# A graph network's first norm and attention product by node blocks, ahead of a run-time branch, with the slot fills spread over the gathers

## The chip, the cores and the metric

The kernel runs on one core of one Trainium2 chip. The metric is the device time of one execution in microseconds (us). The engines are PE (TensorE, matrix products), DVE (VectorE), ACT (ScalarE), POOL (GpSimd) and SP (SyncE, which here only issues DMAs). Each engine works through its own list of instructions in order; waits between engines go over semaphores.

## What is computed

The reference is a stack of four pairs of a graph layer and a feed-forward layer over 3125 nodes of width 256 and 50000 edges sorted by destination. The change touches the first pair and the start of the second:

```python
x = x + _L0_gnn_ref(_layernorm(x, axis=-1), edge_index, L0_gnn_W, L0_gnn_att_src, L0_gnn_att_dst, ...)
x = x + _L0_ffn_ref(_layernorm(x, axis=-1)[None], L0_ffn_router_w, L0_ffn_w1, ...)[0]
x = x + _L1_gnn_ref(_layernorm(x, axis=-1), edge_index, edge_attr_64, L1_gnn_W1, ...)
...
# the first graph layer (8 heads of 32):
h = (x @ W).reshape(n, H, C)
a_src = jnp.einsum('nhc,hc->nh', h, att_src)
a_dst = jnp.einsum('nhc,hc->nh', h, att_dst)
e = a_src[src] + a_dst[dst]
e = jnp.where(e > 0, e, NEG_SLOPE * e)
...
alpha = ex / denom[dst]
msg = h[src] * alpha[..., None]
out = jax.ops.segment_sum(msg, dst, num_segments=n).reshape(n, H * C) + bias
```

## The kernel before, in words

Nodes lie in 25 tiles of 128 (`NT`), grouped in 7 blocks of four tiles, the last block of one (`BLOCKS`). Edges lie in 392 tiles of 128 (`ET`), worked in 28 groups of 14 (`GF`). A tile `x` of all nodes (25 x 256 floats in each of 128 partitions) stays in SBUF for the whole kernel.

The order of the first 700 us is this:

1. **Constants and loads.** x is loaded with two DMAs on SP's queue (L113, L114), the edges' node numbers and weights on ACT's queue (L122, L124).
2. **The flag** (L151 to L195). A fast form of the kernel holds if the edges' destinations fall into expected windows and the source nodes' counts into expected bounds. DVE works this out from the node numbers; for each of 26 node tiles it compares (L181) and ACT squares and sums (L182). The answer is `flag`, one integer.
3. **The first norm** (`layernorm(x, xn)`, `norm_tiles`): statistics of all 25 tiles (L244, L245), one chain of root and reciprocals for all (L226 to L237), then 25 scalings (L248).
4. **The branch.** Every engine reads `flag` (L2095), and the kernel goes on in the form for windows (`gat_gelu`, `mpnn_buckets`, and so on) or in a general form.
5. **`attention`**, in the branch: all of `xn` is transposed by PE (L262), multiplied by `W` (L738), copied to `hs` (L739); the scores of source and destination come from DVE by multiplying `hs` with the attention vectors and summing each head (L744, L746, five tiles at a time). The softmax's shift and the node's own edge follow (L751 to L762). `hs`, 264 floats a node (256 values and 8 scores), is stored in HBM as the table `h_tab` by one DMA (L763).
6. **Fills.** `zero_slots` writes zeros over `slot_x` (10.4 MB, one DMA, L198) and two edges of `rows_y` (L201); `zero_buckets` writes zeros over 25 pieces of `slot_r` (L207). All on SP's queue. `slot_x` is first written with data in the experts that follow, `slot_r` in `mpnn_buckets`.
7. **The edge groups** (`gat_gelu`). For each group POOL gathers the source rows from `h_tab`, 14 indirect DMAs (L293, tile `gw_m`, three buffers); SP loads the row of destination numbers (`dst_hot`, tile `w_row`, L397, one buffer); DVE makes 0/1 matrices of it (L405); PE fetches destination scores with them (L413); ACT and DVE make and apply the weights (L1045 to L1053); PE sums over edges into a window's nodes (L1070). At a node tile's first window its own row from `hs` is weighted and added (L1064 to L1069). Finished nodes get their norm and the router's choice (`consume`).
8. **The experts** (`sparse_experts`): 50 indirect stores into `slot_x`, then 32 tiles of 256 slots, each with two products, results scattered to `rows_y`. In the later expert layers (`sure=43`, `sure=34`) the last tiles are run only if a count read at run time asks for them.
9. **`mpnn_buckets`**: `prepare` takes the experts' two rows for each node of a block (`collect`, tile `se_g`, four tiles at a time, one buffer), adds them, norms and transposes; then edge groups are computed and POOL stores them into `slot_r` with 392 indirect DMAs.

A scheduler fixes the order of each engine's list when the kernel is built: among the instructions of a stretch without a branch it can put one ahead of another that stands earlier in the text, if its inputs are ready sooner. It does not move instructions over the branch. `issue_after` is an explicit edge against that, used in `sparse_experts`.

Of the kernel before, what the change touches and what calls it, by code (L numbers as in the profile page):

```python
# [8 lines left out]
F32 = mybir.dt.float32  # L9
# [8 lines left out]
P = 128  # L18
# [73 lines left out]
def gnn_ffn_kernel(ctx: ExitStack, tc: tile.TileContext, I: dict, out: bass.AP):  # L92
# [20 lines left out]
    nc.sync.dma_start(x[:, :NT - 1], I["x"][:(NT - 1) * P].rearrange("(t p) d -> p t d", p=P))  # L113
# [36 lines left out]
    with tc.tile_pool(name="win", bufs=1) as p, tc.tile_pool(name="win_ps", bufs=1, space=PSUM) as ps:  # L150
        wid = p.tile([P, ET], F32, name="win_w")  # L151
        for k in ("src", "dst"):
            colf[k] = p.tile([P, ET], F32, name=k + "_colw")
            V.tensor_copy(colf[k], col[k])
        for a, b, ts in RUNS:
            nc.gpsimd.memset(dloc[:, a:b], float(ts[0] * P))
            nc.gpsimd.memset(wid[:, a:b], float(len(ts) * P))
        V.tensor_tensor(dloc, colf["dst"], dloc, op=OP.subtract)
        V.tensor_tensor(wid, dloc, wid, op=OP.is_lt)
        V.scalar_tensor_tensor(wid, dloc, 0.0, wid, op0=OP.is_ge, op1=OP.mult)  # L160
        ok = p.tile([P, 1], F32, name="win_ok")
        V.tensor_reduce(ok, wid, AX.X, OP.min)
        col1 = p.tile([P, 1], F32, name="win_1")
        V.memset(col1, 1.0)
        pt = ps.tile([1, 1], F32, name="win_p")
        PE.matmul(pt, ok, col1, start=True, stop=True)
        okf = p.tile([1, 1], F32, name="win_f")
        V.tensor_scalar(okf, pt, P - 0.5, None, op0=OP.is_gt)


        V.tensor_scalar(stile, colf["src"], 1.0 / P, -(P - 1.0) / (2.0 * P), op0=OP.mult, op1=OP.add)
        V.tensor_scalar(stile, stile, 1.5 * 2.0 ** 23, 1.5 * 2.0 ** 23, op0=OP.add, op1=OP.subtract)
        nc.gpsimd.iota(wid, pattern=[[P, ET]], base=0, channel_multiplier=1, allow_small_or_imprecise_dtypes=True)
        V.tensor_scalar(wid, wid, E - 0.5, float(NT), op0=OP.is_ge, op1=OP.mult)
        V.tensor_tensor(stile, stile, wid, op=OP.max)
        V.scalar_tensor_tensor(sloc, stile, -float(P), colf["src"], op0=OP.mult, op1=OP.add)
        V.tensor_scalar(sloc, sloc, 1.0, None, op0=OP.add)
        rt = p.tile([P, NT + 1], F32, name="win_rt")
        for b in range(NT + 1):
            eq = p.tile([P, ET], F32, name="win_eq", bufs=3)  # L180
            V.tensor_scalar(eq, stile, float(b), None, op0=OP.is_equal)  # L181
            S.activation(eq, eq, AF.Square, accum_out=rt[:, b:b + 1])  # L182
        po, pc = (ps.tile([P, NT + 1], F32, name="win_p" + k) for k in "oc")
        PE.matmul(pc, ones, rt, start=True, stop=True)
        PE.matmul(po, upper, rt, start=True, stop=True)
        V.scalar_tensor_tensor(sadj, iota256[:, :NT + 1], float(BT * P), po, op0=OP.mult, op1=OP.add)
        V.tensor_scalar(sadj, sadj, -1.0, None, op0=OP.add)
        lo, hi = p.tile([1, NT], F32, name="win_lo"), p.tile([1, NT], F32, name="win_hi")
        for a, b in ((0, NT - 1), (NT - 1, NT)):
            V.tensor_scalar(hi[:, a:b], pc[0:1, a:b], B_TILES[a] * P + 0.5, None, op0=OP.is_lt)  # L190
            V.tensor_scalar(lo[:, a:b], pc[0:1, a:b], B_FULL[a] * P - 0.5, None, op0=OP.is_gt)
        V.tensor_tensor(lo, lo, hi, op=OP.mult)
        V.tensor_reduce(hi[:, 0:1], lo, AX.X, OP.min)
        V.tensor_tensor(okf, okf, hi[:, 0:1], op=OP.mult)
        V.tensor_copy(flag, okf)  # L195

    def zero_slots():
        nc.sync.dma_start(slot_x.rearrange("(a p) w -> p a w", p=P),  # L198
                          zero[:, :D + 1].unsqueeze(1).to_broadcast([P, SLOTS // P + 1, D + 1]))
        for k in range(2):  # L200
            nc.sync.dma_start(rows_y[k * NR + N:(k + 1) * NR], zero[:NR - N, :D])  # L201

    def zero_buckets(slot_r):
        for b in range(NT):
            n = B_TILES[b] - B_FULL[b]
            row = (b * BT + B_FULL[b]) * P
            nc.sync.dma_start(slot_r[row:row + n * P].rearrange("(k p) w -> p k w", p=P),  # L207
                              zero[:, :D + 1].unsqueeze(1).to_broadcast([P, n, D + 1]))

# [413 lines left out]
    def sparse_experts(hot, n, T, name, f, act, beside=iter(()), meanwhile=None, sure=None):  # L623
# [83 lines left out]
        def collect(pool, t0, nt):  # L707
            g = pool.tile([P, len(hot), 4, D], F32, name="se_g")[:, :, :nt]
# [14 lines left out]


    def attention(p, h_tab):


        hs = p.tile([P, NT, W], F32, name="hs")
        ad = p.tile([P, NT, 16], F32, name="ad")
        exs = p.tile([P, NT, 8], F32, name="exs")  # L730
        w = load_w(p, "L0_gnn_W")
        with transposed(xn), tc.tile_pool(name="gat_ps", bufs=3, space=PSUM) as ps, \
                tc.tile_pool(name="gat_t", bufs=2) as tp:
            att = {k: load_bc(tp, "L0_gnn_" + k, D) for k in ("att_src", "att_dst")}
            for t in range(NT):
                pt = ps.tile([P, D], F32, name="gat_p")
                for c in range(2):
                    PE.matmul(pt, xnT[:, c, t * P:(t + 1) * P], w[:, c], start=c == 0, stop=c == 1)  # L738
# [1462 lines left out]
```

## Time and profile before

| what | value |
|---|---|
| time, median of 3 runs | 5363.52 us (5352.59 to 5365.13) |
| the profiled execution, its own time | 5371.22 us |
| its span, first to last instruction | 5369.5 us |
| granted TensorE clock, mean | 0.844 |
| busy, share of the span: PE, DVE, POOL, ACT | 79%, 48%, 42%, 22% |
| DMA | 644.19 MB, mean 120 GB/s |
| gathers of `gw_m` on POOL | 392, 401.2 us busy, 1024 ns mean |
| SP's first `zero_slots` store issued; wait of the next one (L201) behind it | 38.38 us; 44.1 us |
| first load of `se_g` in `mpnn_buckets` | 915.18 us |

A row of the timeline gives start, duration, engine, line, operation, output and input tiles and a count; in brackets stands how long the engine was idle before it and what released it. A row by stretches gives the length, each engine's busy time with its instruction count, the granted TensorE clock, the DMA engines' busy share and GB/s. "issue" as releaser means that the profile shows nothing that was waited for. L12 is line 12 of the kernel.

### The profile page before, as it was taken

How to read it: one execution, taken by the hardware profiler on the slowest of the kernel's cores; microseconds unless marked ns; L12 is line 12 of the kernel's file. 1: busy time of each engine (PE TensorE's matmuls, PEld its weight loads, DVE VectorE, ACT ScalarE, POOL GpSimd, SP SyncE). 2: the span in 40 equal slices, each digit the busy share in tenths (PEclk: the TensorE clock that was granted, in tenths of full speed). 3: DMA queues.
4: the chain of work that ended last, by engine and by line, in shares of the span. 5: the costliest groups of instructions: out<-in, count | busy, mean ns of one | idle time of the engine just before them, and what ended most of it. 6: DMA issues, size and time to landing. Idle time of an engine off the chain costs nothing. (4 is left out here: it accounts for less than half of the span.)

```text
span 5369.5 us, 59465 instructions
## 1 busy us (share of the span) xinstructions
PE 4264.2 (79%) x19362; PEld 2844.8 (53%) x19362; DVE 2594.7 (48%) x9507; ACT 1176.0 (22%) x2327; POOL 2245.9 (42%) x2372
## 2 busy tenths in 40 slices
PE   2578738999979999583799999989787788775694
PEld 2466527455556666442566666655454344443483
DVE  6577637311144555436856766762333313336324
ACT  2001012222233333111333433453000100002121
POOL 1777644767710000133523333300777537771521
PEclk8778859888989999756899999998788758885797
DMA  7644437545442232144333333312333223330564
GB/s 200 198 151 150 129 110 235 188 141 166 163 140 71 89 98 79 32 150 134 121 95 104 104 106 96 96 44 85 107 104 105 77 73 104 104 105 21 174 214 135
DMA packets 338232, 644.19 MB, mean 120 GB/s; under 512 B 54675, under 2 KB 244087, under 8 KB 333559
## 3 DMA queue, kind: packets, MB, share of 16 engines
q1 hardware_dynamic: 219872, 335.77, 20.1%
q0 software_dynamic: 108480, 298.44, 18.2%
q10 hardware_dynamic: 9558, 6.01, 0.4%
q8 instruction: 163, 2.67, 0.2%
q14 instruction: 159, 1.29, 0.1%
HBM read 508.81 MB, written 131.23 MB: 119 GB/s over the span
## 5 line engine op out<-in xcount | busy, mean ns | idle before, releaser
L293 POOL DMA_INDIRECT hc_wm<-hc_tabc,src_col x784 | 749.3, 956 | 649.2 <-DMA w_L_gnn_c_w<-in_L_gnn_c_w 304.0
L377 PE MATMUL w_acc<-hc_wm,w_eq 128*128 128x256 f32 x2208 | 751.4, 467 | 203.7 <-DMA hc_wm<-hc_tabc,src_col 148.4
L377 PEld LDWEIGHTS w_acc<-hc_wm,w_eq 128*128 128x128 f32 x2208 | 438.9, 224 | 516.7 <-DVE w_eq L370 258.8
L370 DVE TENSOR_SCALAR w_eq<-iota,dloc,ew 128x128 f32<-128x128 f32 (+1 forms) x784 | 300.3, 385 | 748.0 <-PE w_acc L377 741.1
L293 POOL DMA_INDIRECT hb_r<-hy_x,src_col x392 | 386.4, 986 | 644.3 <-PE hb_acc L1869 390.1
L610 POOL DMA_INDIRECT slot_x<-xn,sl_i x125 | 122.1, 977 | 975.3 <-DVE sl_i L582 754.4
L610 POOL DMA_INDIRECT slot_r<-mq_r,bk_i x392 | 399.5, 1019 | 195.5 <-issue 93.5
L293 POOL DMA_INDIRECT gw_m<-gat_h,src_col x392 | 401.2, 1024 | 140.0 <-issue 123.5
L1070 PE MATMUL gw_acc<-gw_m,gw_eqt 128*128 128x264 f32 x1104 | 303.7, 436 | 97.7 <-issue 86.0
L1899 PE MATMUL hb_pc<-hb_parts,w_hot 128*128 128x257 bf16 x1656 | 270.3, 295 | 138.3 <-DVE hbe_a L1904 88.1
L610 POOL DMA_INDIRECT rows_y<-se_y,se_to x175 | 181.3, 1036 | 349.0 <-DVE se_y L694 181.9
L1193 PE MATMUL mq_pe<-a_L_gnn_W1T_c,mq_ea 64*128 64x256 f32 x784 | 300.0, 466 | 29.3 <-ACT mq_r L1195 14.7
L1070 PEld LDWEIGHTS gw_acc<-gw_m,gw_eqt 128*128 128x128 f32 x1104 | 232.6, 216 | 153.4 <-issue 90.2
L413 PEld LDWEIGHTS <-w_hot 128*128 128x128 bf16 x3312 | 187.2, 100 | 233.6 <-issue 197.8
L1869 PE MATMUL hb_acc<-hb_r,hb_eq 128*128 128x257 f32 x1104 | 290.9, 389 | 13.3 <-DVE hb_eq L1864 13.2
L1899 PEld LDWEIGHTS <-w_hot 128*128 128x128 bf16 x1656 | 159.9, 103 | 264.3 <-DVE hbe_a L1904 125.8
L413 PE MATMUL mq_pe<-mq_q,w_hot 128*128 128x256 bf16 x1656 | 272.8, 294 | 0.0
L405 DVE TENSOR_SCALAR w_hot<-w_row,node_id 128x1792 bf16<-128x1792 int32 (+13 forms) x183 | 151.7, 833 | 218.8 <-PE mq_pe L413 153.1
L1770 ACT ACTIVATE hb_h<-hb_ph,hb_o,hb_s 128x512 f32<-128x512 f32 (+1 forms) x224 | 162.7, 730 | 413.0 <-PE hb_ph L1768 412.8
L1869 PEld LDWEIGHTS hb_acc<-hb_r,hb_eq 128*128 128x128 f32 x1104 | 200.4, 194 | 76.7 <-issue 27.5
L688 PE MATMUL se_py<-se_w,se_h 128*128 128x256 f32 (+1 forms) x886 | 236.3, 412 | 1.1 <-ACT se_h L681 1.0
L679 PE MATMUL se_ph<-se_xT,se_w 128*128 128x256 f32 (+1 forms) x972 | 235.8, 392 | 0.5 <-DVE se_xT L662 0.5
(523 smaller groups left out, 7266.9 us busy)
## 6 DMA issues: line engine op xcount, KB each, us to landing
w_row<-in_dst_row SPq DMA_DIRECT2D x84, 896.0 KB, 5.2
mb_r<-slot_r SPq DMA_DIRECT2D x48, 1156.5 KB, 5.7
se_w<-in_L_ffn_lanes SPq DMA_DIRECT2D x34, 1026.0 KB, 5.4
hb_w<-in_L_ffn_W SPq DMA_DIRECT2D x112, 256.0 KB, 2.7
se_r<-slot_x SPq DMA_DIRECT2D x66, 257.0 KB, 3.6
se_w<-in_L_ffn_lanes SPq DMA_DIRECT2D x32, 513.0 KB, 5.0
se_g<-rows_y SPq DMA_DIRECT2D x30, 512.0 KB, 5.7
hb_w<-in_L_ffn_Wo SPq DMA_DIRECT2D x56, 256.0 KB, 2.8
```

Of the source, the lines that this page charges most:

```text
L293: nc.gpsimd.indirect_dma_start(out=dst, out_offset=None, in_=table, in_offset=bass.IndirectOffsetOnAxis(ap=idx, axis=0))
L370: V.tensor_scalar(eq[:, :n], iota256[:, :n], dloc[:, i:i + 1], scale[:, u:u + 1], op0=OP.is_equal, op1=OP.mult)
L377: PE.matmul(acc[t][:, :width], eq[:, k * P:(k + 1) * P], m[:, u, :width], start=i == W_FIRST[t], stop=i == W_LAST[t])
L413: PE.matmul(o, hot[t][:, u * P:(u + 1) * P], parts[:, t, k, :width], start=start and j == 0, stop=j == len(ops) - 1)
L610: d = nc.gpsimd.indirect_dma_start(out=table, in_=rows, in_offset=None, out_offset=bass.IndirectOffsetOnAxis(ap=idx, axis=0)).ins
L679: PE.matmul(ph[:fp], w[:, c * f + j * P:c * f + j * P + fp], xT[:, c], start=c == 0, stop=c == 1)
L688: PE.matmul(py[:, u], h[:kp, j, u * P:(u + 1) * P], w[:kp, o2 + j * D:o2 + (j + 1) * D], start=j == 0, stop=j == nj - 1)
L1070: PE.matmul(acc[t][:, :W], eq[:, k * P:(k + 1) * P], m[:, u], start=False, stop=i == W_LAST[t])
L1193: PE.matmul(pt[:, v], ea[:, (u + v) * P:(u + v + 1) * P], w1c, start=True, stop=False)
L1770: S.activation(o[:, j, :n], ph[:, :n], AF.Relu, bias=shift[i][:, e, j:j + 1], scale=scale[i][:, e, j:j + 1])
L1869: PE.matmul(acc[t][:, :D + 1], eq[:, k * P:(k + 1) * P], b[:, u], start=i == W_FIRST[t], stop=i == W_LAST[t])
L1899: PE.matmul(pc[:, :D + 1], hot[t][:, u * P:(u + 1) * P], parts[t][:, 0, k], start=z == 0, stop=z == len(ops) - 1)
```

## The change

x comes in seven DMAs, six of four tiles and the last part tile. The flag's work becomes a generator, `windows`, that stops at seven places. `attention` now stands ahead of the branch and goes over the blocks: norm of four tiles, transposes, product, copies, one store of the block's rows into the table, and after each block but the first two steps of the flag's work. The attention scores come out of the same product: the weight `W` is extended by 16 columns, `W` times the heads' vectors, made by PE at the start from the transposed weight and a block matrix laid out on the host. `hs` is not kept in SBUF; a node tile's own row is loaded again from the table. The fills become generators too: `slot_x` in 21 pieces of up to four tiles and `slot_r` in 25, one of each for each edge group. In `mpnn_buckets` the experts' rows are collected two tiles at a time. `ad` and `exs` (scores and own weights) live to the end of the kernel.

```diff
-    nc.sync.dma_start(x[:, :NT - 1], I["x"][:(NT - 1) * P].rearrange("(t p) d -> p t d", p=P))
+    for t0 in range(0, NT - 1, 4):
+        nc.sync.dma_start(x[:, t0:t0 + 4], I["x"][t0 * P:(t0 + 4) * P].rearrange("(t p) d -> p t d", p=P))
...
     def zero_slots():
-        nc.sync.dma_start(slot_x.rearrange("(a p) w -> p a w", p=P),
-                          zero[:, :D + 1].unsqueeze(1).to_broadcast([P, SLOTS // P + 1, D + 1]))
+
         for k in range(2):
             nc.sync.dma_start(rows_y[k * NR + N:(k + 1) * NR], zero[:NR - N, :D])
+        per = 4
+        for a in range(0, SLOTS // P + 1, per):
+            n = min(per, SLOTS // P + 1 - a)
+            nc.sync.dma_start(slot_x[a * P:(a + n) * P].rearrange("(a p) w -> p a w", p=P),
+                              zero[:, :D + 1].unsqueeze(1).to_broadcast([P, n, D + 1]))
+            yield
...
             nc.sync.dma_start(slot_r[row:row + n * P].rearrange("(k p) w -> p k w", p=P),
                               zero[:, :D + 1].unsqueeze(1).to_broadcast([P, n, D + 1]))
+            yield
...
-        def collect(pool, t0, nt):
-            g = pool.tile([P, len(hot), 4, D], F32, name="se_g")[:, :, :nt]
+        def collect(pool, t0, nt, size=4):
+            g = pool.tile([P, len(hot), size, D], F32, name="se_g")[:, :, :nt]
...
+    def windows(p, ps):
...
+        for b in range(NT + 1):
+            eq = p.tile([P, ET], F32, name="win_eq", bufs=3)
+            V.tensor_scalar(eq, stile, float(b), None, op0=OP.is_equal)
+            S.activation(eq, eq, AF.Square, accum_out=rt[:, b:b + 1])
+            if b % 4 == 3:
+                yield
...
-    def attention(p, h_tab):
...
+    h_tab0 = tc.dram_tile([NR, W], F32, name="gat_h")
+    ad = const.tile([P, NT, 16], F32, name="ad")
+    exs = const.tile([P, NT, 8], F32, name="exs")
+
+    def attention(beside):
...
+            w = p.tile([P, 2, D + 16], F32, name="at_w")
+            nc.scalar.dma_start(w[:, :, :D], I["L0_gnn_W"].rearrange("(k p) c -> p k c", p=P))
+            wT, heads = load_w(p, "L0_gnn_WT"), load_w(p, "L0_gnn_heads", 2, 16)
+            for k in range(2):
+                pt = pbt.tile([P, 512], F32, name="bt_p")
                 for c in range(2):
+                    PE.matmul(pt[:, :16], wT[:, c, k * P:(k + 1) * P], heads[:, c], start=c == 0, stop=c == 1)
+                V.tensor_copy(w[:, k, D:], pt[:, :16])
+            sc = p.tile([P, NT, 8], F32, name="at_sc")
+            for s, n in BLOCKS:
+                t0, nt = s // P, n // P
+                norm_tiles(bp, x, xn, t0, nt)
+                xT = block_transposed(bp, pbt, xn, t0, nt, "at_xT")
+                hs = bp.tile([P, 4, W], F32, name="at_hs")
+                for u in range(nt):
+                    pt = ps.tile([P, 512], F32, name="at_p")
+                    for c in range(2):
+                        PE.matmul(pt[:, :D + 16], xT[:, c, u * P:(u + 1) * P], w[:, c], start=c == 0, stop=c == 1)
+                    S.copy(hs[:, u], pt[:, :W])
+                    S.copy(ad[:, t0 + u, :8], pt[:, W:W + 8])
+                nc.sync.dma_start(node_rows(h_tab0)[:, t0:t0 + nt], hs[:, :nt])
+                V.tensor_copy(sc[:, t0:t0 + nt], hs[:, :nt, D:])
+                for _ in range(2 if s else 0):
+                    next(beside, None)
+            for _ in beside:
+                pass
...
     def gat_gelu(mp, slot_r, beside):
...
-                hs, ad, exs = attention(p, h_tab)
-                zero_slots()
-                zero_buckets(slot_r)
...
+                    fills = [zero_slots(), zero_buckets(slot_r)]
...
                         hot = dst_hot(ep, g, 1)
+                        for fill in fills:
+                            next(fill, None)
...
                                     own = bp.tile([P, W], F32, name="gw_own")
+                                    nc.sync.dma_start(own, h_tab[t * P:(t + 1) * P])
                                     V.tensor_tensor(own[:, :D].rearrange("p (h c) -> p h c", h=HEADS),
-                                                    hs[:, t, :D].rearrange("p (h c) -> p h c", h=HEADS),
+                                                    own[:, :D].rearrange("p (h c) -> p h c", h=HEADS),
...
-                g = collect(tp, t0, nt)
-                for u in range(nt):
-                    add(t0 + u, g[:, :, u])
+                for u0 in range(0, nt, 2):
+                    m = min(2, nt - u0)
+                    g = collect(tp, t0 + u0, m, 2)
+                    for u in range(m):
+                        add(t0 + u0 + u, g[:, :, u])
...
-    layernorm(x, xn)
+    with tc.tile_pool(name="win", bufs=1) as p, tc.tile_pool(name="win_ps", bufs=1, space=PSUM) as ps:
+        attention(windows(p, ps))
     in_windows = nc.values_load(flag[0:1, 0:1], min_val=0, max_val=1)
```

## The prediction

> **What bounds the kernel now.** I read the table by 50 us stretches first, then the timeline of the first 190 us, then SP's and POOL's waits, and last the stretch 898 to 1012 us, because the change also touches a load there. The page gives the span.
>
> ```profile
> span 5369.5 us, 59465 instructions
> ```
>
> By stretches (length, busy us of PE, PE loads, DVE, ACT, POOL with instruction counts, then granted clock, DMA share, GB/s):
>
> ```profile
> 50.00:100.00 50.00, 31.66 (x150) 27.41 (x150) 41.65 (x70) 14.34 (x33) 0.00 (x0) 0.85 0.86 222
> 100.00:150.00 50.00, 3.27 (x6) 1.55 (x6) 22.72 (x47) 0.37 (x1) 26.27 (x24) 0.53 0.96 275
> 150.00:200.00 50.00, 21.03 (x159) 17.48 (x160) 21.57 (x46) 1.13 (x4) 29.82 (x32) 0.62 0.68 209
> 186.00:648.00 462.00, 357.59 (x2819) 289.07 (x2815) 343.10 (x965) 43.46 (x96) 355.59 (x350) 0.83 0.50 154
> ```
>
> From 186 to 648 us POOL issues gathers without a break: it counts as 77% busy, but each 0.95 us gather is followed by a fixed 0.30 us, so it is full. PE (358/462 = 77%) and DVE (343/462 = 74%) are not. **POOL's 392 gathers set this stage**, and whatever lets the first one start earlier, or removes a hole in their row, comes off the end. The timeline shows what precedes them:
>
> ```profile
> 37.21 0.14 DVE L195 CAST flag<-win_f 1x1 int32<-1x1 f32 x1
> 37.44 0.75 DVE L244 BATCH_NORM_STATS2 ln_st<-x 128x6 f32<-128x256 f32 x2
> 104.72 1.49 DVE L746 TENSOR_REDUCE ad<-gat_tmp 128x40 f32<-128x1280 f32 x1
> 104.88 0.36 SPq L763 DMA_DIRECT2D gat_h<-hs  x1
> 105.29 50.34 SPq L207 DMA_DIRECT2D slot_r<-zero  x20
> 117.20 1.39 POOL L293 DMA_INDIRECT gw_m<-gat_h,src_col  x1 [9.95 <-DMA gat_h<-hs]
> 118.89 5.05 POOL L293 DMA_INDIRECT gw_m<-gat_h,src_col  x1 [0.30 <-issue]
> 155.81 16.29 SPq L397 DMA_DIRECT2D w_row<-in_dst_row  x2
> 170.57 1.15 DVE L405 TENSOR_SCALAR w_hot<-w_row,node_id 128x1792 bf16<-128x1792 int32 x1 [47.46 <-DMA w_row<-in_dst_row]
> 186.08 0.94 POOL L293 DMA_INDIRECT gw_m<-gat_h,src_col  x1 [11.04 <-issue]
> 647.58 0.95 POOL L293 DMA_INDIRECT gw_m<-gat_h,src_col  x1 [0.30 <-issue]
> ```
>
> The flag, the norm and the attention run one after another to 106 us, the table of 3.3 MB lands at 117. Then SP sits in the zero fills until 155.8, so the first row of node numbers (`w_row`), in program order behind the fills, makes DVE wait 47 us. POOL fills its three group buffers (42 gathers, the last at 174.10) and stops for 11.04 us. From 117.20 to 647.58 is 530.4 us for 391 steps. Undisturbed (186.08 to 647.58, 349 steps) a step takes 461.5/349 = 1.322 us, so 391 steps need 517.0: 13.4 us of the stage are holes, those 11 and the slow 5.05 us gather.
>
> **The change, part by part.** *The stretch before the gathers.* Removed: ten multiplies and ten reductions of 1.49 us (DVE rows L744, L746; issued 1.40 us apart, 28 us from 78.17 to 106.1), the wait of the norm for the flag, and the wait for the whole norm. Added: PE columns 256 to 272, 25 small ACT copies, 7 instead of one table stores, and small norm steps seven times. What each engine then has to do, from the rows:
> - DVE: statistics 10.0 (37.44 to 47.4), applying 8.2 (L248, 25 in 8.16), the chain of root and reciprocal 1.5 for each of 7 blocks (49.28 to 50.61 and 0.18) = 10.6, seven score copies of 0.2 = 1.4, the flag's work 16.7 (5.7 before the 26 compares, 26 x 0.36 = 9.4, tail 1.6). Sum 47.
> - ACT: 26 squares 13.4 (L182), 7 roots 1.5, 14 transposed copies 7.5, 25 copies of 0.37 = 9.3, 25 small ones of about 0.2 = 5, three table loads 3.8. Sum 40.5.
> - PE: 50 transposes 9.9 (L262, 3.06 + 6.88), products 22.4 (L738, 2.42 + 20.02) x 272/256 = 23.8, the weights' heads some 2. Sum 36 at the 0.9 clock of 60 to 80 us; at the 0.53 of 100 to 117, 36 x 0.9/0.53 = 61.
>
> These now overlap. DVE had its first column list at 3.77 and `dst` at 6.99, so a first part of x is there at about 6: 6 + 47 = 53 if DVE never waits. Behind its last part come one tile's transposes, copies, product and copy (0.7 + 1.0 + 0.9 + 0.6 = 3.2), the store (2 to 4; the 128 KB and 256 KB rows land in 2.2 to 2.8) and the branch (SP's first fill came 1.0 after the flag): **61 at best**. At worst PE bounds at half clock: the identity is there at 12.0, 12 + 61 + 7 = 80, and another 12 for the seven handovers DVE to ACT to DVE to PE to ACT (the same serial chain took 678.2 to 688, 10 us, for one block): **92**. I take 73, nearer the first: the busiest engine holds 47, and the flag's 16.7 us are there to fill the gaps. Gain 117.2 - 73 = **44.2** (bounds 25 to 56).
>
> The root alternates with the flag's squares on ACT. The row decides that this needs no table loads: the 125 squares of L1588 stand among roots and show none. The Trainium skill ("ScalarE: Activation LUTs", "Table sets: the hidden batching unit") says to batch by set and names relu, copy, identity and abs as present in all, not the square; by it, with its 2.66 us a switch, 14 switches would put 37 us on ACT and make it the bound, near my 92.
>
> The 16 to 25 bias additions that DVE now does while it waits move behind the branch; they have the 18 us before the first group is complete.
>
> *The fills.* 21 pieces of slot_x and 25 of slot_r (514 KB each but one) move from one burst to two a group. The first `w_row` comes before them in the program, so the 11 us stop and the slow second gather go: 530.4 becomes 517.0. The same 23 MB still pass SP: twenty pieces took 50.34 us beside gathers, 2.5 each. If the scheduler bunches them, `w_row` waits 2.5 for each piece ahead of it, and up to the old 13.4 comes back. I allow 3. Gain **10.4** (0 to 13.4). Bytes are no obstacle: two pieces in 18.5 us add 57 GB/s to the 154 there, and 275 was moved in 100 to 150 while gathers kept 1.25 us apart. Here the Trainium skill speaks against the change: "DMA: Bandwidth & Descriptors" ("Bandwidth") wants 1 MiB or more for 75% of peak. Big and small fills show little of it here: the stretches show 344 GB/s at 40 to 44 us with the single 10.4 MB fill and 313 at 130 to 156 with pieces and gathers; by the rule the sum would lose a few us more of the 10.4.
>
> *Own rows.* 25 loads of 132 KB replace reading SBUF. The 128.5 KB loads of L656 land in 2.3 us; SP can issue them one tile ahead, two buffers exist, and DVE and PE have 26% and 23% slack, 4.8 us of a group. Taken at 0; uncovered 25 x 2.3 = 57.
>
> *Experts' rows in two halves.* `collect` in `mpnn_buckets` now loads two tiles at a time into one buffer. For the first block the second load waits for the first's additions: the additions ran from 919.09 and loads take 3.8 at least, so +**4**, which the first POOL scatter (937.74) inherits. Later blocks are ahead of need: DVE waits there 7.4 to 7.75 us a group for POOL's scatters. Uncovered, six blocks add 6 x 3.8 = 23.
>
> *Split x load, constants kept for good*: nothing beyond the above.
>
> Sum: -44.2 - 10.4 + 4 = **-50.6**. The profiled execution took 5371.22 (span 5369.5), 7.7 above the median of 5363.52; so 5320.6 for it, and 5363.5 - 50.6 = **5313** for the median.
>
> **Rivals.** *Half is given back* (5339): the stretch ends at 92 and the holes stay: -25.2 - 0 + 4 = -21, 5342; with the holes half gone, 5336. For it: PE's clock was 0.53 when it worked in bits. Against: before, PE was at 0.94 within 10 us of its first transpose. *More is gained* (5297): start at 61, no hole: -56.2 - 13.4 + 4 = -65.6. Needs an almost unbroken DVE. *Own rows stall the stage* (slower): SP is one queue in order, and its waits at `w_row` sum to 158.8 us in 12 (13.2 each) behind DVE's compares alone. If each own row stands behind such a wait, DVE stops 25 x 13.2 = 330 us; 28 groups x 4.8 = 134 absorb the first part, 196 stay: 5313 + 196 = 5509. It decides from (134 + 50.6)/25 = 7.4 us a tile. Against: SP's list is built by readiness (it put the slot_x fill of L198 ahead of the earlier-written store L763), so own rows should go early. *Empty tiles passed over*: the diff holds no such code. `sure=43` and `sure=34` with their `If` are in both kernels, the first experts keep all 32 tiles; worth 0, already in the sum.
>
> **How the numbers follow.** Main case 0.68 (own range 5297 to 5330), more gained 0.11, half given back 0.14, stall 0.04, other scheduling in the rest that eats it all 0.03 (5360). The range 5288 to 5342 leaves out the stall, that last case and the edges, 2 in 10. Noise is about 0.3% = 16 us: faster means below 5347. Faster 0.91, same 0.05, slower 0.04.
>
> **What would show it.** First gather near 73 (61 to 92) and after the flag's cast; no `gat_tmp` rows; no POOL hole over 5 us in the first 60 us of gathers; `w_row` landed within 10 us of the first gather; last gather near 593; steps still 1.32 us; the first scatter of slot_r some 4 us later after the last rows_y scatter than before. Wrong if steps exceed 1.45, if DVE waits for `gw_own` loads, or if stages past 1000 us change length.

## The result, and the profile after

| | before | changed |
|---|---|---|
| median of 13 runs each, taken together | 5377.44 us (5342.88 to 5418.81) | 5325.73 us (5272.48 to 5353.44) |
| profiled execution, its span | 5369.5 us | 5315.8 us |
| granted clock of the profiled execution | 0.844 | 0.848 |

The ratio is 0.9898, with a 95% interval of 0.9867 to 0.9929: 1.0% less, some 55 us, and the interval excludes no change. The medians above differ by 51.7 us, since the ratio leaves out one execution of the changed kernel, that of 5353.44 us, which fell in a slower state. The prediction's 5313 against its 5363.5 is a ratio of 0.9906. The profiled execution took 5317.6 us.

The two traces by stages (start of the first instruction of a kind, us):

| mark | before | changed | difference |
|---|---|---|---|
| first gather of `gw_m` | 117.20 | 68.61 | -48.6 |
| last gather of `gw_m` | 647.58 | 596.65 | -50.9 |
| first scatter into `slot_x` | 710.27 | 659.59 | -50.7 |
| first load of `se_g` | 915.18 | 864.53 | -50.7 |
| first scatter into `slot_r` | 937.74 | 893.93 | -43.8 |
| last scatter into `slot_r` | 1507.54 | 1455.37 | -52.2 |
| end of the span | 5369.5 | 5315.8 | -53.7 |

Nearly all of the gain is made before the first gather. By stretches, the kernel after (length, busy us of PE, PE loads, DVE, ACT, POOL with instruction counts, then granted clock, DMA share, GB/s):

```profile
20.00:40.00 20.00, 18.33 (x81) 13.61 (x80) 18.67 (x81) 16.58 (x66) 0.54 (x1) 1.00 0.20 70
40.00:50.00 10.00, 9.03 (x44) 7.45 (x44) 5.49 (x29) 9.73 (x41) 0.00 (x0) 1.00 0.23 79
50.00:68.00 18.00, 6.98 (x31) 4.77 (x30) 9.66 (x44) 5.50 (x18) 0.59 (x1) 0.83 0.38 121
180.00:225.00 45.00, 24.70 (x225) 20.47 (x224) 29.86 (x87) 5.22 (x9) 32.11 (x31) 0.73 1.06 327
225.00:597.00 372.00, 292.06 (x2274) 233.64 (x2273) 277.15 (x803) 34.60 (x78) 285.17 (x280) 0.86 0.53 162
```

Between 20 and 50 us PE, DVE and ACT now work at the same time, at a clock of 1.00. From 225 us on, the gathers are alone with their stage's own traffic (162 GB/s); just before, the fills bring the DMA share to 1.06. The timeline of the kernel after:

```profile
51.58 0.13 DVE L733 CAST flag<-win_f 1x1 int32<-1x1 f32 x1
60.01 0.34 SPq L767 DMA_DIRECT2D gat_h<-at_hs  x1
67.06 0.56 DVE L350 CAST gw_ap<-sp_r 128x400 bf16<-128x400 f32 x1
68.61 1.30 POOL L253 DMA_INDIRECT gw_m<-gat_h,src_col  x1 [7.15 <-DMA b_L_gnn_ln_w<-in_L_gnn_ln_w]
76.97 1.14 DVE L365 TENSOR_SCALAR w_hot<-w_row,node_id 128x1792 bf16<-128x1792 int32 x1
224.39 0.96 POOL L253 DMA_INDIRECT gw_m<-gat_h,src_col  x1 [4.06 <-issue]
596.65 0.95 POOL L253 DMA_INDIRECT gw_m<-gat_h,src_col  x1 [0.30 <-issue]
```

The table's last store is issued at 60.01; the first gather comes 8.6 us later, right behind DVE's split of the scores (`sp_r`, done at 67.6). The first compare with `w_row` comes 8.4 us after the first gather, where it waited 47 us before. The longest idle time of POOL among the gathers is 4.06 us, at 224 us, where the last of the fills are on their way; another of 2.09 us follows at 227 us.

Twelve runs followed, in four sets, each on a chip of its own (b to e; each row below is one profile). The times are single executions but for e11 and e12 (medians of 6 and 10), so no verdict on the whole kernel hangs on them; in the first row they are the medians of 13. On chip b the kernel before took 5447 us in its one execution; on c, d and e 6203 to 6258 us, and there the gather row is 701 to 741 us long in every kernel, the changed one included. So the rows of those chips are not compared; the stretch before the first gather and the interval from the first `slot_x` scatter to the first `slot_r` scatter are, since the unaltered parts agree on all chips (first gather 67.6 to 70.3, interval 232.0 to 234.4). The kernel before was profiled in the first comparison alone.

| run | chip | time | first gather | row, first to last gather | `slot_x` to `slot_r` |
|---|---|---|---|---|---|
| before / changed, first comparison | - | 5377.4 / 5325.7 | 117.2 / 68.6 | 530.4 / 528.0 | 227.5 / 234.3 |
| e1_spread | b | 5337.2 | 68.4 | 524.0 | 234.1 |
| e2_burst | b | 5377.4 | 67.6 | 592.1 | 233.7 |
| e3_splitmem | b | 5356.5 | 64.1 | 533.8 | 234.4 |
| e4_headsact | b | 5336.6 | 68.1 | 530.2 | 232.0 |
| e5_inbranch | c | 6172.6 | 96.9 | (712.1) | 234.3 |
| e6_dvescores | c | 6161.1 | 91.7 | (711.9) | 232.6 |
| e7_winfirst | c | 6132.1 | 76.5 | (730.4) | 234.2 |
| e8_collect_ab | c | 6185.2 | 68.8 | (704.5) | 234.3 |
| e9_row_first | d | 6145.0 | 70.3 | (734.1) | 233.5 |
| e10_ad_wide | d | 6208.4 | 69.7 | (741.3) | 234.0 |
| e11_mended | e | 6129.4 | 62.2 | (702.6) | 227.8 |
| e12_changed | e | 6143.2 | 68.7 | (701.2) | 232.8 |

### The profile page after: what moved, and what is told of

It is laid out like the page before. It is cut to its first block, busy times and chain, and to the rows that moved or that the text cites. A ratio compares the mean times of both kernels' runs of the same rounds, so it can differ in the third digit from the quotient of the medians.

```text
span 5315.8 us, 59675 instructions
## 1 busy us (share of the span) xinstructions
PE 4261.4 (80%) x19370; PEld 2837.0 (53%) x19370; DVE 2560.1 (48%) x9525; ACT 1177.9 (22%) x2364; POOL 2243.8 (42%) x2372
## 5 line engine op out<-in xcount | busy, mean ns | idle before, releaser
L1095 PEld LDWEIGHTS gw_acc<-gw_m,gw_eqt 128*128 128x128 f32 x1104 | 232.6, 217 | 190.5 <-issue 94.1
L373 PEld LDWEIGHTS <-w_hot 128*128 128x128 bf16 x3312 | 182.9, 99 | 192.9 <-issue 155.6
L373 PE MATMUL mq_pe<-mq_q,w_hot 128*128 128x256 bf16 x1656 | 265.0, 288 | 0.4 <-DVE mq_q L1202 0.4
L641 ACT ACTIVATE se_h<-se_ph,se_w 128x256 f32<-128x256 f32 (+1 forms) x243 | 110.1, 454 | 550.3 <-PE se_ph L639 373.8
```

Of the source, the lines that this page charges most:

```text
L373: PE.matmul(o, hot[t][:, u * P:(u + 1) * P], parts[:, t, k, :width], start=start and j == 0, stop=j == len(ops) - 1)
L1095: PE.matmul(acc[t][:, :W], eq[:, k * P:(k + 1) * P], m[:, u], start=False, stop=i == W_LAST[t])
```

## Experiments on the stretch before the first gather

**What the first gather waits for.** The wait at 68.61 is put down to a small load that nothing here needs. My reading: the gathers' buffer lies in the memory that the split's scratch has just used.

```diff
-                with tc.tile_pool(name="gw_s", bufs=1) as tp:
-                    split3(tp, a_parts, ad)
+                split3(p, a_parts, ad)
```

> The changed kernel with the scratch tile of the split (sp_r) in memory of its own, so that the first gather's buffer is not the memory that the split has just used. Theory (in the changed kernel the first gather at 68.61 us waits for the split, whose last instruction ends at 67.62): first gather at 64 to 66.5 us, every later stage earlier by the same 2 to 4.5. Rival (the gather waits for the table's store and the branch): first gather stays within 0.7 us of 68.6.

Timeline of this run:

```profile
64.11 1.39 POOL L253 DMA_INDIRECT gw_m<-gat_h,src_col  x1 [1.53 <-SPq L2229]
67.88 0.56 DVE L350 CAST gw_ap<-sp_r 128x400 bf16<-128x400 f32 x1
220.20 0.96 POOL L253 DMA_INDIRECT gw_m<-gat_h,src_col  x1 [3.94 <-issue]
223.24 0.95 POOL L253 DMA_INDIRECT gw_m<-gat_h,src_col  x1 [2.08 <-issue]
265.20 1.01 POOL L253 DMA_INDIRECT gw_m<-gat_h,src_col  x1 [7.40 <-issue]
```

The gather now starts before the split ends, 3.0 us after the table's last store is issued (61.13): the theory held, 4.5 us earlier. In the changed kernel and in the five altered ones of this part that keep the shared memory, the first gather comes some 1 us after the split's end (in e5, 95.44 + 0.57 = 96.0 and 96.92). But the second half of the expectation failed: the last gather came at 597.87, no earlier than 596.65. The row grew to 533.8, the more so in groups 6 to 9 (1.555 and 1.607 us a step): POOL idles at 220 us as in the changed kernel, and a further 7.40 us at 265. The last fill is issued at 231.22 instead of 222.65, and a compare at 244.45 has waited 7.53 us for a `w_row` issued at 230.83, behind a run of fills. So the fills are likely to have taken back what was won at the start; this run alone doesn't show it.

**Which engine sets the stretch.** The prediction took DVE, with 47 us of work the largest sum.

```diff
-                V.tensor_copy(w[:, k, D:], pt[:, :16])
+                S.copy(w[:, k, D:], pt[:, :16])
```

> The changed kernel with the two copies of the product of the weights with the attention heads on ACT instead of DVE, so that DVE does not wait 4.4 us for them (9.0 to 13.4 us) ahead of its statistics. Theory (DVE's row of work sets the stretch to the first gather, so that an early stop of it is paid in full): first gather 3 to 5 us earlier, 63.5 to 66. Rival (ACT, PE or the flag's chain sets it, DVE has slack in the stretch): within 1 us of 68.6, or later by the two copies on ACT.

First gather at 68.05, 0.6 us earlier: the rival. DVE did more before 40 us (32.69 instead of 29.47 us busy), yet the flag is cast at 51.02 instead of 51.58. So I looked at ACT; of its groups in the first 70 us of the changed kernel, these (busy us and mean ns of one, then idle time before them):

```profile
L718 ACT ACTIVATE win_eq<-win_eq 128x392 f32<-128x392 f32 x26 | 14.1, 552 | 0.0
L765 ACT COPY at_hs<-at_p 128x264 f32<-128x264 f32 x25 | 9.5, 388 | 5.8 <-PE at_p L764 5.6
...
L766 ACT COPY ad<-at_p 128x8 f32<-128x8 f32 x25 | 4.6, 186 | 0.0
L186 ACT ACTIVATE ln_s<-ln_e 128x4 f32<-128x4 f32 (+1 forms) x7 | 1.5, 225 | 10.3 <-DVE ln_e L195 10.3
L186 ACT ACT_TABLE_LOAD x1 | 1.3, 1283 | 4.4 <-DMA src_col<-in_src_col 4.4
```

ACT is full from 23.7 to 49 us, and the roots of the last two blocks stand in its list behind the flag's squares: the first of the two inputs is ready at 40.72 on DVE, both roots start at 49.16.

```diff
-                hs = bp.tile([P, 4, W], F32, name="at_hs")
+                hs = bp.tile([P, 4, W + 8], F32, name="at_hs")
...
-                    S.copy(hs[:, u], pt[:, :W])
-                    S.copy(ad[:, t0 + u, :8], pt[:, W:W + 8])
+                    S.copy(hs[:, u], pt[:, :W + 8])
...
+                V.tensor_copy(ad[:, t0:t0 + nt, :8], hs[:, :nt, W:])
```

> The changed kernel with ACT's 25 small copies of the target scores (0.17 us each, 0.27 apart, some 6 us in all) replaced by 8 more columns in the big copy and one DVE copy a block. Theory (ACT is the full engine of the stretch, back to back from 23.7 to 49 us, and holds the roots of the last two blocks some 8 us in its queue; taking 4 to 6 us from it is paid): first gather 2.5 to 6 us earlier, 62.5 to 66. Rival (DVE, or the flag's chain, sets it): within 1.5 us of 68.6.

69.66, and e9 on the same chip, the same up to there, had 70.26: 0.6 us for 4.6 us less on ACT. But this run doesn't decide. The scheduler put the pieces in another order, in which PE waits 2.14 us for a norm up to 44.77, and behind that wait its granted clock falls to 0.50 from 45.27 to 52.10 us, where the changed kernel has 1.00 from 24.48 to 62.03. The same stretch, e10 and then the changed kernel (columns as above):

```profile
45.50:52.00 6.50, 6.04 (x15) 4.33 (x16) 4.07 (x20) 2.96 (x9) 0.00 (x0) 0.50 0.01 3
```

```profile
45.50:52.00 6.50, 4.57 (x22) 3.76 (x22) 2.94 (x25) 4.43 (x20) 0.00 (x0) 1.00 0.38 134
```

One block's products take 6.49 us there instead of 3.93 (657 ns each instead of 392), and e9 in its turn has 0.50 from 52.99 to 56.40. What ACT's 4.6 us are worth at an equal clock stays open. DVE's wait is not what sets the stretch (e4, whose clock is 1.00 from 23.13 to 60.68, as in the changed kernel); which engine or order does is not shown.

The granted clock is thus part of every figure of this section. It fell after some pauses of PE and not after others: pauses of 1.65 to 1.66 us near 50 us are followed by 3.4 us at 0.50 in e3 and e9, and by none in the changed kernel.

**The order in the text.**

```diff
             sc = p.tile([P, NT, 8], F32, name="at_sc")
+            for _ in beside:
+                pass
...
-                for _ in range(2 if s else 0):
-                    next(beside, None)
-            for _ in beside:
-                pass
```

> The changed kernel with the flag's work written out whole ahead of the first block, instead of two of its pieces after each block; all of it is still ahead of the branch. Theory (DVE takes work in the order in which it is written, so the 16.7 us of flag work go ahead of the first block): first gather 8 to 17 us later, 77 to 86. Rival (what can overlap is found by readiness, the interleaving in the text is not needed): within 4 us of 68.6.

76.49 against 68.76 on the same chip (e8): 7.7 us. The flag is cast at 38.16, 13 us earlier, and the products end later. It lies half a us under the theory's range and far from the rival's: the scheduler overlaps much by itself, not all. PE stands from 26.51 to 35.85 here and its clock is 0.50 from 29.84 to 40.08, which is in the 7.7 us.

**The score columns.**

```diff
...
-                        PE.matmul(pt[:, :D + 16], xT[:, c, u * P:(u + 1) * P], w[:, c], start=c == 0, stop=c == 1)
-                    S.copy(hs[:, u], pt[:, :W])
-                    S.copy(ad[:, t0 + u, :8], pt[:, W:W + 8])
+                        PE.matmul(pt[:, :D], xT[:, c, u * P:(u + 1) * P], w[:, c, :D], start=c == 0, stop=c == 1)
+                    S.copy(hs[:, u, :D], pt[:, :D])
+                for k, o in (("att_src", hs[:, :nt, D:]), ("att_dst", ad[:, t0:t0 + nt, :8])):
+                    tmp = bp.tile([P, 4, D], F32, name="gat_tmp")[:, :nt]
+                    V.tensor_tensor(tmp, hs[:, :nt, :D], att[k].unsqueeze(1).to_broadcast([P, nt, D]), op=OP.mult)
+                    V.tensor_reduce(o, tmp.rearrange("p t (h c) -> p t h c", h=HEADS), AX.X, OP.add)
```

> The changed kernel with the two scores of a node computed on DVE again (multiply by the attention vector, then a reduction, one pair for each vector and block, 14 multiplies and 14 reductions of up to 1.49 us, 37 us in all, instead of 16 extra columns in the product). Theory (the prediction's: DVE's 47 us are the largest of the three sums and set the stretch, so its 28 us of score work paid in full): first gather 20 to 30 us later, 88 to 99. Rival (the handovers of seven blocks set the stretch at some 6.4 us a block and DVE has 10 to 20 us of slack in them): 5 to 17 us later, 74 to 86. Second rival: under 4 us later.

91.71, 23.0 us later than e8 on the same chip. That is the theory's range: 30.8 us of multiplies and reductions come back, and DVE is busy for 32.80 us of the first 40 and 25.82 of the next 28. Taking them away was worth 23 us, not the whole of their work; some of it is PE's clock, which falls to 0.50 three times here (34.36 to 41.19, 48.01 to 54.84 and 65.08 to 75.32 us), after PE's waits. In the changed kernel DVE is no longer the limit (e4).

**The place ahead of the branch.**

```diff
-        attention(windows(p, ps))
+        for _ in windows(p, ps):
+            pass
...
     with tc.If(in_windows == 1) as branch:
+        attention(iter(()))
...
```

> The changed kernel with the flag's work ahead of the branch and the attention, still by node blocks, inside it: the price of the move ahead of the branch alone. Theory (most of the 48.6 us of the first gather's gain is the overlap of flag, norm and products): the flag is cast near 37 us as in the kernel before, the branch comes some 1 us later, the norm of 7 blocks may run before it but attention only after it; the first gather comes 14 to 30 us later, at 83 to 98 us. Rival (it is the blocks and the score columns that pay, the place of the branch is worth little): first gather within 6 us of 68.6. The gather row itself unchanged at 524 to 532.

96.92, 28.2 us later, inside the theory's range. The flag is cast at 36.82, and the norm starts at 38.27. More than the place changes, though: behind the branch SP issues fills at once, the first at 38.56 and 18 of the 46 ahead of the last two stores of the table (84.66 and 86.63), and the granted clock is 0.50 up to 55.99. So a part of the 28.2 may be theirs. The prices of e5, e6 and e7 overlap and don't add up to 48.6.

## Experiments on the fills

**All fills in one burst, ahead of the first `w_row`.**

```diff
+                for fill in (zero_slots(), zero_buckets(slot_r)):
+                    for _ in fill:
+                        pass
...
-                    fills = [zero_slots(), zero_buckets(slot_r)]
...
-                        for fill in fills:
-                            next(fill, None)
```

> The changed kernel with its fills issued in one burst ahead of the first w_row again, all else as changed: the price of the fills' place alone. Theory: the first gather stays at 68 to 70 us; 46 pieces of about 2.5 us end near 61 + 46 x 2.5 = 176 us at worst, 61 + 75 = 136 if only the slot_x pieces and some of slot_r go first; the first w_hot comes at 125 to 180 us, POOL fills its three buffers (42 gathers, to about 68.6 + 42 x 1.3 = 123) and then stops for 11 to 60 us; the gather row is 540 to 575 us instead of 528.0. Rival (the place of the fills is worth nothing, the holes of 13.4 us that the prediction counted are set by something else): the row stays within 3 us of 528.

SP's, DVE's and POOL's lines of this run:

```profile
60.41 50.55 SPq L158 DMA_DIRECT2D slot_x<-zero  x21
111.01 56.67 SPq L166 DMA_DIRECT2D slot_r<-zero  x25
...
168.23 1.03 SPq L357 DMA_DIRECT2D w_row<-in_dst_row  x1
```

```profile
180.54 1.15 DVE L365 TENSOR_SCALAR w_hot<-w_row,node_id 128x1792 bf16<-128x1792 int32 x1 [93.13 <-DMA w_row<-in_dst_row]
```

```profile
122.90 0.95 POOL L253 DMA_INDIRECT gw_m<-gat_h,src_col  x1 [0.30 <-issue]
195.52 0.95 POOL L253 DMA_INDIRECT gw_m<-gat_h,src_col  x1 [71.67 <-PE gw_acc L1095]
```

46 pieces hold SP for 107 us, 2.33 each; `w_row` is issued only at 168.23, DVE waits 93 us, POOL fills its three buffers up to 122.90 and stops for 71.7. The row is 592.1, 64 us longer and above the expected range. The place of the fills is worth 64 us in the changed kernel; in the kernel before, the hole was only 11.04 because the one big `slot_x` fill had run under the attention. With the burst the last gather comes at 659.72, 12 us later than in the kernel before in the first comparison, in spite of a start 50 us earlier: at this mark the burst takes the whole of the earlier start. (As a whole e2 took 5377 us where the kernel before took 5447 on the same chip, one execution each; with no profile of the latter the two marks can't be compared there.) By the Trainium skill ("DMA: Bandwidth & Descriptors", "Bandwidth") transfers should be 1 MiB or larger for 75% of the peak; here the 514 KB pieces keep the queues at a DMA share of 1.09 and 291 GB/s beside the gathers (68 to 120 us), and no run here tried larger ones in this place.

**Fills tied to their group.** In the changed kernel the text has two fills a group, but the scheduler issued all 46 between 61 and 224 us, up to fourteen after one `w_row`, the last five of them all of `slot_r`.

```diff
...
-                        for fill in fills:
-                            next(fill, None)
+                        with tc.issue_after(row_load.ins):
+                            for fill in fills:
+                                next(fill, None)
```

> The changed kernel with one thing altered: the two fills of a group are ordered behind that group's load of w_row, so that they can no longer be bunched. Theory (the bunched fills, 46 pieces between 61 and 224 us, keep the gather row at 528.0 us where 391 steps at 1.322 are 517): the row from the first to the last gather shrinks to 518 to 521 us, no two-group mean over 1.42 us a step among groups 0 to 9, fills seen on SP until past 400 us; the span some 8 us shorter. Rival (the early holes come from DVE, PE or the own rows and the fills are innocent): the row stays within 2 us of 528. Second rival (thin fills now fall between later w_row loads and delay those): the row grows, 530 or more, with holes after 240 us.

The last fill is now issued at 522.6. By stretches, this run:

```profile
180.00:225.00 45.00, 23.78 (x243) 19.58 (x241) 27.88 (x86) 6.30 (x11) 33.00 (x32) 0.73 0.66 186
225.00:592.00 367.00, 292.26 (x2229) 233.61 (x2229) 272.85 (x787) 33.52 (x76) 282.43 (x276) 0.85 0.69 200
```

The DMA share between 180 and 225 us falls from 1.06 to 0.66, and what is moved after 225 rises from 162 to 200 GB/s. Groups 6 and 7 take 1.382 us a step, against 1.481 in the changed kernel and 1.555 and 1.468 in e3 and e4, and POOL's idle time near 220 us is 3.0 us instead of 6.1. The row is 524.0, against 528.0, 533.8 and 530.2 in the three kernels with bunched fills, one profile each. So the bunch makes about half of that hole, and is worth some 4 to 10 us. But neither 517 nor the expected 518 to 521 is reached. Groups 0 and 1 take 1.376 us a step, no better than 1.380 in e3 with its fills bunched (1.471 in the changed kernel, 1.411 in e4, 1.421 before): the slow first groups are not the bunch. Past group 10 the mean step is 1.337, against 1.325 to 1.335 in the bunched three, too little to say whether thin fills cost something there.

## Experiments on the experts' rows in halves

The interval from the first `slot_x` scatter to the first `slot_r` scatter grew from 227.5 to 234.3 us. The prediction's reason was that the second load waits for the first's additions.

```diff
...
-                for u0 in range(0, nt, 2):
-                    m = min(2, nt - u0)
-                    g = collect(tp, t0 + u0, m, 2)
-                    for u in range(m):
-                        add(t0 + u0 + u, g[:, :, u])
+                for u in range(nt):
+                    g = collect(tp, t0 + u, 1, 1, "se_g" + "ab"[u % 2])
+                    add(t0 + u, g[:, :, 0])
```

> The changed kernel with the experts' rows of a block loaded one tile at a time into two buffers by turns instead of two tiles at a time into one; the same memory, the same bytes. From the first scatter of slot_x to the first scatter of slot_r took 227.5 us before and 232.1 to 234.4 in the changed kernel and the three runs that share this part. Theory (the second load of the first block waits for the additions of the first): the interval falls to 228 to 231. Rival (something else in the stage, such as the order of the loads on SP, makes the 6 us): it stays at 232 to 235.

234.28: no help. That alone doesn't clear the second load, since the third load now waits for a buffer, and `w_row`, next on SP's queue, is issued 5.4 us after the first load, as late as in the changed kernel (5.8; 1.6 before). DVE's timeline in the changed kernel shows what the norm waits for:

```profile
874.73 0.17 DVE L195 TENSOR_SCALAR ln_e<-ln_mv 128x4 f32<-128x4 f32 x1
879.40 1.15 DVE L365 TENSOR_SCALAR w_hot<-w_row,node_id 128x1792 bf16<-128x1792 int32 x1 [4.51 <-DMA w_row<-in_dst_row]
880.47 0.17 DVE L188 RECIPROCAL ln_r<-ln_s 128x4 f32<-128x4 f32 x1
```

The same place in the kernel before:

```profile
924.34 0.17 DVE L235 TENSOR_SCALAR ln_e<-ln_mv 128x4 f32<-128x4 f32 x1
924.78 0.18 DVE L228 RECIPROCAL ln_r<-ln_s 128x4 f32<-128x4 f32 x1 [0.27 <-ACT ln_s L226]
...
925.47 1.15 DVE L405 TENSOR_SCALAR w_hot<-w_row,node_id 128x1792 bf16<-128x1792 int32 x1
```

The sums are done 9.2 us after the first load of `se_g` before, and 10.2 after the change: the halves themselves cost 1.0. The reciprocal comes 9.6 and 15.9 us after it: the other 5.3 are the compare with `w_row`, which now stands ahead of the norm in DVE's list and waits for its DMA, issued 4.2 us later than before behind the second load. First try, the load of `w_row` earlier:

```diff
...
+                    row = hot_row(ep, g)
                     ahead = WIN[min((g + 2) * GF, ET) - 1][-1]
                     while blocks and blocks[0][0] <= ahead * P:
                         prepare(*blocks.pop(0))
...
-                    hot = dst_hot(ep, g)
+                    hot = dst_hot(ep, g, row=row)
```

> The changed kernel with the loads of w_row in the stage of slot_r issued ahead of the experts' rows (se_g) of a block. From the first scatter of slot_x to the first of slot_r took 227.5 us before, 232.1 to 234.4 in the changed kernel, and 234.3 with the experts' rows in two buffers by turns, so the prediction's reason (the second load waits for the additions) has fallen. New theory (the halves only put w_row behind the second load: w_row is issued 870.35 - 864.53 = 5.8 us after the first se_g load instead of 1.6, and DVE, whose next instruction is the compare with it, stands 4.5 us ahead of the norm's reciprocal): the interval falls to 228 to 231. Rival (the stage is late for the bytes or the norm itself): it stays at 232 to 235.

233.5: no help. The scheduler then put the compares further ahead still: DVE waits 4.23 us for `w_row` in front of the first additions and 2.65 for the next row in front of the second. An earlier load doesn't help if the list asks for it earlier too. Second try, in the run with all mends: the order on DVE itself.

## All mends together, beside the changed kernel

```diff
... (the fills as in e1)
-                with tc.tile_pool(name="gw_s", bufs=1) as tp:
-                    split3(tp, a_parts, ad)
+                split3(p, a_parts, ad)
...
-                    hot = dst_hot(ep, g)
+                    with nullcontext() if g else tc.issue_after(normed.ins):
+                        hot = dst_hot(ep, g)
```

> The changed kernel with three mends together, each read from its own stage: fills ordered behind w_row, scratch of the split in memory of its own, and the first compare with w_row in the slot_r stage ordered on DVE behind the first block's norm (it stood ahead of it, with two orders of the loads alike). Theory: first gather at 64 (with the second alone: 64.11); gather row 521 to 527, since fills behind w_row gave 524.0, so the last gather at 585 to 591 where the changed kernel has 596.65; from the first slot_x scatter to the first slot_r scatter 228 to 231 us instead of 232 to 234.4. Sum 5 + 5 to 8 + 4: 12 to 17 us less than the changed kernel on the same chip. Rival (the earlier start is eaten by the fills, as it was with the split's memory alone, 533.8 us for the row; the compare is not what delays the norm): last gather within 3 us of 596, interval 232 to 235, the time within 0.1% of the changed kernel.

> The changed kernel itself, for the comparison with the mended one on the same chip and to see how far its stages vary: first gather 68 to 70 us, gather row 526 to 530 and first slot_x to first slot_r scatter 232 to 235 us if the chip is like that of the first comparison; ratio to the kernel before 0.987 to 0.993.

The mended kernel's DVE at that place:

```profile
1047.21 0.17 DVE L195 TENSOR_SCALAR ln_e<-ln_mv 128x4 f32<-128x4 f32 x1
1047.65 0.18 DVE L188 RECIPROCAL ln_r<-ln_s 128x4 f32<-128x4 f32 x1 [0.27 <-ACT ln_s L186]
...
1050.15 1.15 DVE L369 TENSOR_SCALAR w_hot<-w_row,node_id 128x1792 bf16<-128x1792 int32 x1
```

No compare stands between the sums and the reciprocal of the first block any more, which comes 10.3 us after the first load of `se_g` (1037.31). The interval is 227.8, against 232.8 in the changed kernel on the same chip: 5.0 us, close to the 5.3 that the compare was read to cost. The first gather came at 62.20 against 68.74, 6.5 us earlier, more than the 4.5 of e3: both come 3.0 us after the last store of the table, but e3, with its clock at 0.50 from 53.44 to 56.85, issued that store at 61.13 and e11 at 59.22. The last gather came only 5.1 us earlier (764.85 and 769.99), on a chip where the row is not set by POOL.

As a whole the gain can't be told from nothing there: the ratio to the kernel before is 0.9879 (0.9841 to 0.9918) for the mended and 0.9871 (0.9832 to 0.9909) for the changed kernel, medians 6129.38 and 6143.19 us. The changed kernel's own ratio of the first comparison (0.9898) lies inside. That the mends are worth the 12 to 17 us expected is not shown; that the split and the compare stall where they were read is. The fills' order can't be seen on this chip (rows of 702.6 and 701.2).

## Why the prediction was right

- **First gather at 73, bounds 61 to 92:** 68.61. Right in size, and so were the sums: in the first 68 us DVE is busy for 44.6 us, PE for 36.9 and ACT for 33.5. The clock, at 1.00 from 24.48 to 62.03, kept the stretch far from the bound of 92, which had PE at half clock. (The reason given, 0.94 within 10 us of the first transpose, was not safe: before, that transpose came at 51.20, and the clock was 0.50 from 58.11 to 64.94.) The largest piece was read right (DVE's score work, 28 us in rows L744 and L746; e6 pays 23.0 to put it back in another form). The assumption that DVE's 47 us go on setting the stretch was not: DVE freed of a wait of 4.4 us wins 0.6 (e4). And "61 at best" counted no wait for the split: it is 62.2 to 64.1 without the shared memory (e11, e3).
- **Root beside squares needs no table load:** right. ACT shows one at 4.4 us, and the next, at 60.07, belongs to the exponential; 26 squares and 7 roots alternate in between. The one load is the root's: the kernel before and e5, where the squares come first, load a table for them at 2.22 and another for the first root (47.73 and 40.74), so the table of the root serves the square here, and the squares' first one did not serve the root. The rule in the Trainium skill ("ScalarE: Activation LUTs", "Table sets: the hidden batching unit") is to batch by set; the square beside the root was no case of it here, the exponential was. A load takes 1283 ns in this trace, and 134 of its 155 loads start within 0.1 us of ACT's last instruction, with the next one 1.31 us behind that (median), half of the 2.66 us a switch by which the 37 us were reckoned.
- **Gather row 520, gain 10.4:** 528.0, gain 2.4. The term that was mis-sized. The hole of 11 us went, as said. But 517 took every step at the undisturbed 1.322 us, and 11.0 us are left over it. 4.2 of them lie in groups 0 and 1: "the slow second gather" was put down to the fills, but the first 28 gathers take 3.5 to 6.2 us more than 0.946 each in all five profiles of the first comparison's and chip b's changed kernels, wherever the fills stand, and 4.5 before. 6.2 lie in groups 6 to 9, with the hole at 224 us; "if the scheduler bunches them" was priced at 3, and e1, without the bunch, takes back 4.
- **Own rows at 0:** DVE waits for `gw_own` twice, 5.2 us together, which the prediction had named as a sign of being wrong. The longer wait (4.78 us, to 199.63) is covered: soon after it DVE stands 7.58 us for gathered rows (to 207.77), without which the work couldn't go on. Right in size.
- **`collect` in halves, +4:** +6.9 at the first `slot_r` scatter. Right in place and sign. The wait that it named is there (the second load is issued 4.9 us after the first), but it costs the sums only 1.0; 5.3 came another way, through `w_row`, held behind that load on SP, and a compare with it that had changed places with the norm. The order alone brings 5.0 back (e11).
- **Sum -50.6:** all three terms lie ahead of the first `slot_r` scatter, and the marks there give -43.8: -48.6 at the start, -2.4 in the row, +6.9 in the collecting, and 0.3 between. So the three errors, 4.4 too little, 8.0 too much and 2.9 too little, left the sum 6.8 too high. From there to the end the changed kernel is 9.9 us shorter, which no term holds. The `slot_r` stage alone took 569.8 before and 561.4 after, but 561.1, 573.5, 578.6 and 596.4 in the four runs on chip b with the same code in it, so that these 9.9 us are within what this stage varies by itself. That the total agrees to 4 us (50.6 against 55 by the ratio, 53.7 between the profiles) is in part such luck.
- **The rivals:** own rows stalling the stage didn't come about. "Half is given back" was nearer for the fills (11.0 us over 517 are left of 13.4), not for the start.

## What to carry to other kernels

When a start is moved forward, look up what next stands on the same queue: here fills in one burst would have cost 64 us, more than the whole of the early start, and a further 4.5 us won at the start were gone again at the last gather (e3). A loop that says "two a group" is not an order; if it matters, it takes an explicit edge behind the load that must go first. And sums of engine work bound a stretch from below only. What is to be looked at near the bound is which instruction stands ahead of which in an in-order list, above all one that waits for a DMA (5 us at one compare here), and whether an engine's pause lowers PE's granted clock (e10).

## What the runs showed of the hardware that I had not expected

On three of the chips the same code takes 6.1 to 6.3 ms instead of 5.3 to 5.45, and the stage of the gathers is where it is seen best. The same stretch, changed kernel, in the first comparison and then on chip e (columns as above):

```profile
300.00:400.00 100.00, 84.58 (x587) 68.22 (x586) 79.90 (x251) 10.83 (x24) 77.15 (x76) 0.86 0.51 153
```

```profile
300.00:400.00 100.00, 57.65 (x391) 46.48 (x392) 56.03 (x157) 6.43 (x15) 53.31 (x55) 0.74 0.36 105
```

A single gather takes POOL the same 0.95 us on both, and the first gather comes at the same time; but 55 gathers are issued in 100 us instead of 76, with idle times of up to 19.6 us in this stretch, and the DMA engines move 105 GB/s at a share of 0.36 where they move 153 at 0.51. POOL no longer bounds the stage there, and the DMA engines are less busy too. Late gathers are not what the traces show: between 100 and 770 us DVE waits 94.5 us for gathered rows ahead of the weights (L1069) in the first comparison, and at most 25 in any profile of chips c, d and e. Instead PE stops between plain products that stand ready in its list (L373), 97.3 us in 77 stops on chip e and 61 to 100 us in every profile of these chips, with nothing in the profile that it waited for; in the first comparison there is none of it. DVE, too, stands ahead of L1069 for something that the profile doesn't name (29.89 us once in e8 on chip c). The granted clock of these chips is lower as well (0.77 to 0.79 over the span, 0.84 to 0.85 in the first comparison). What makes PE stop was not tried.
